# Residual loads, step order and a power on GpSimd at the seam between a mamba layer and an attention layer

## The chip, the cores and the metric

The kernel runs on 1 core of a Trainium2 chip. The metric is the device time in microseconds (us) of one execution. Engines in the profile: PE (TensorE: matmuls; PEld its weight loads), DVE (VectorE), ACT (ScalarE), POOL (GpSimd), SP (SyncE, which here only issues DMAs). Each engine works through its own queue in the order in which the program lists its instructions; between engines, semaphores order them.

## The reference, cut to what matters

Input `x` is 8 images of 128 channels and 64 x 64 pixels, in float32; an image is 4096 tokens of 128 numbers. Two layers are computed.

```
# layer 0: a mamba block, then group norm, silu and the residual
t = tokens(x); t = mamba(t)
x = silu(group_norm(image(t))) + x
# layer 1: additive attention, then a mixture of experts
t = tokens(x)
t = t + attn(layernorm(t))     # w[i,j] = exp(sum_a w2[a] tanh(f[i,a]+g[j,a]+b1[a]) + b2), j < i, normalised over j
t = t + moe(layernorm(t))      # each of 64 experts takes its 8 best tokens of an image
```

`layernorm` subtracts the mean of a token's 128 numbers and multiplies by (variance + 1e-5) to the power -0.5.

## The kernel before, in words

The work is cut into 64 chunks of 512 tokens, 8 an image (`NC` is 64, `NCH` is 8). Instructions run in the order in which the program is written (a manual schedule), so the order of the calls is the order on every queue.

**Mamba** (`mamba`) is a software pipeline over chunks: step p works on up to nine chunks in different stages. Late stages of a chunk c, which matter here, are: `normal` (group norm and silu on `o`), `again` (L434: a DMA that loads the input chunk once more, as the residual `xr`, 256 KB, two buffers), `turn` (L446, L449: transposes of `o` and of `xr` on PE, added in PSUM), `taken` (L456: ACT copies the sum to `tt`, two buffers), `moments` (L460 stores `tt` to `k_dram` by SP; L465 to L468 are the statistics on DVE), `spread` (L472, L473: logarithm and exponential on ACT, which make the power -0.5), `centre` (L478, DVE), `tokens` (L490, DVE, makes the normalised `tok`, two buffers; L486 the same on ACT for earlier chunks), `turn_back` (PE transposes `tok` back, L501 ACT copies that to `xT`, L502 a small POOL memset sets a column of `tok` to one), `vectors` (L507 stores `tok` to `k_dram` by SP; L516 two matmuls; L518 to L520 two exponentials and a scaled copy on ACT, which make `uv`) and `save` (L523: `uv` to `uv_dram`, 768 KB, by SP).

**The passage**: when the last chunk has left the scan, `remaining` (L559 to L576) finishes the late stages of the last chunks, steps p = 68 to 78. In step p, c5 to c10 are chunks p - 11 and p - 12 to p - 15. In three of the steps it calls `bring(0, g)`, which loads what attention needs of chunk g of image 0: sixteen DMAs of 64 KB for `U` and `V` (L826, L827) and two of 256 KB for `tt` and `tok` (L831). For the first three chunks the sixteen are issued by POOL, else by SP. `aw` is attention's pool of buffers, `mw` that of mamba; they share memory.

**Attention** (`attend`) walks 1056 tiles of keys by queries, 132 an image. Iteration i has several tiles in flight: `rounds` (L718, 32-row matmuls into denominators D of tile i+3 and numerators N of tile i), `logarithms` (L728, L729: ACT takes the logarithm of D), `inverses` (L735: one ACT exponential over tile i+2's reciprocals and tile i-1's scores), `ratios` (L740, three DVE products), `scores` (L753 on DVE, then L754 on POOL, whose sum L735 exponentiates in the next iteration), `causal` (L746, a mask on POOL), `weigh` (L766, matmuls). Work on finished rows (`finish`, `route`, `choose`) is written as generators that yield an engine kind and a cost; `advance` lets a few steps of them run in each iteration, between `causal` and `scores` for those on DVE and ACT. `route` calls `normalise`, once a chunk (64 times): L792 to L796 are the statistics on DVE, L798 and L799 the logarithm and the exponential on ACT (128 x 4 numbers), L802 applies them in later steps on DVE. After the tile loop come the experts and the output.

Of the kernel before, what the change touches and what calls it, by code (L numbers as in the profile page):

```python
# [9 lines left out]
F32 = mybir.dt.float32  # L10
AF = mybir.ActivationFunctionType
ALU = mybir.AluOpType
AX = mybir.AxisListType

P = 128
CH = 512
# [46 lines left out]
def fast_path(  # L63
# [24 lines left out]
    nc = tc.nc  # L88
    B = x.shape[0]
    L = x.shape[2] * x.shape[3]  # L90
    NCH = L // CH
    NB = L // P
    NQ = CH // P
    NC = B * NCH
    xf = x.rearrange("b c h w -> b c (h w)")
# [7 lines left out]
    def fixed(name, *shape):  # L103
        return const.tile(list(shape), F32, name=name)

    ident, ones = fixed("ident", P, P), fixed("ones", P, P)
# [8 lines left out]
    gamma, beta, gateb = fixed("gamma", P, 1), fixed("beta", P, 1), fixed("gateb", P, 1)  # L115
    wuv, biasv, wcol = fixed("wuv", P, 2, P), fixed("biasv", P, 1), fixed("wcol", P, 1)
    back, shift, tiny = fixed("back", P, P + 1), fixed("shift", P, 1), fixed("tiny", P, 1)
    floor = fixed("floor", P, 1)
    gwide = fixed("gwide", P, 3 * NE)

    def halves(queue, t, src):
# [2 lines left out]
    def prepare(mw, bank):  # L124
# [33 lines left out]
        spread = mw.tile([P, 2, NR, CH], F32, tag="rep", bufs=2, name="prep_spread")  # L158
        spread = spread.rearrange("p r n t -> p (r n t)")[:NS, : NS * P].rearrange("p (a r) -> p a r", a=NS)
# [55 lines left out]
        nc.vector.tensor_scalar(tiny, tiny, 1e-10, None, ALU.mult)  # L215
        nc.vector.memset(shift, -SHIFT)
        nc.vector.memset(floor, EPS)
        nc.vector.tensor_reduce(gsel, ident.rearrange("p (g c) -> p g c", c=GROUP), AX.X, ALU.add)
        nc.vector.tensor_scalar(
            gmean3, gsel.unsqueeze(2).to_broadcast([P, P // GROUP, GROUP]), 1.0 / GROUP, None, ALU.mult  # L220
# [9 lines left out]
    k_dram = [dram.tile([2, P, CH], F32, name=f"k_dram{c}", tag=f"k{c}") for c in range(NC)]  # L230
# [9 lines left out]
    def mamba(mw, small, psum):  # L240
# [5 lines left out]
        ch = [{} for _ in range(NC)]  # L246
# [255 lines left out]
            nc.gpsimd.memset(k[:, :, P - 1 : P], 1.0)  # L502
            ch[c]["ones"] = k

        def vectors(c, late=None):
            xT = ch[c].pop("xT")
            nc.sync.dma_start(k_dram[c][1], ch[c].pop("ones").rearrange("p q c -> p (q c)"))  # L507
            if late is None:
                puv = psum.tile([P, 2, CH], F32, tag="pz", name=f"puv{c}")
                puv = [puv[:, s, :] for s in range(2)]  # L510
                uv = mw.tile([P, 3, CH], F32, tag="uv", bufs=1, name=f"uv{c}")
            else:
                puv = [psum.tile([P, CH], F32, tag=f"px{s}", name=f"puv{c}_{s}") for s in range(2)]
                uv = late.tile([P, 4, CH], F32, tag="mix", bufs=5, name=f"uv{c}")[:, :3]
            for s in range(2):
                nc.tensor.matmul(puv[s], lhsT=wuv[:, s, :], rhs=xT, start=True, stop=True)  # L516
            ch[c]["uv"] = uv
            nc.scalar.activation(uv[:, 0, :], puv[0], AF.Exp, bias=shift)  # L518
            nc.scalar.activation(uv[:, 1, :], puv[1], AF.Exp, bias=biasv)
            nc.scalar.activation(uv[:, 2, :], uv[:, 1, :], AF.Copy, scale=wcol)  # L520

# [33 lines left out]
        def on(c, step, *args):  # L555
            if c is not None:
                step(c, *args)

        def remaining(aw, bring):  # L559
            for p in range(NC + 4, NC + NCH + 7):  # L560
                c5, c7, c8, c9, c10 = (
                    p - i if 0 <= p - i < NC else None for i in (NCH + 3, NCH + 4, NCH + 5, NCH + 6, NCH + 7)
                )
                if p > NC + 4:
                    on(c10, save)
                on(c8, moments)
                on(c8, spread)
                on(c8, centre)
                on(c8, tokens)
                on(c9, vectors, aw)  # L570
                on(c7, turn)
                on(c7, taken)
                on(c8, turn_back)
                on(c5, again)
                if p % 2 == 0 and p - NC - 4 < 6:
                    bring(0, (p - NC - 4) // 2)  # L576

        setup = prepare(mw, lambda h, name: psum.tile([P, CH], F32, tag=f"da{h}", name=name))
        load(0)
        next(setup)  # L580
        load(1)
        for p in range(NC + 4):

            c1, c2, c3, c4, c5, c7, c8, c9, c10 = (
                p - i if 0 <= p - i < NC else None
                for i in (0, 1, 2, 3, NCH + 3, NCH + 4, NCH + 5, NCH + 6, NCH + 7)
            )
# [63 lines left out]
            nc.scalar.preload_act_table_set(LOG_EXP)  # L651
            on(c8, turn_back)
            on(c9, vectors)
            next(setup, None)
        save(NC + 3 - (NCH + 6))
        return remaining

    def attend(aw, small, ap, remaining):
# [20 lines left out]
        U, V, tok, tt, lnf = {}, {}, {}, {}, {}  # L679
# [104 lines left out]
        def normalise(n, src, dst):  # L784

            st = small.tile([P, NQ, 6], F32, tag="st", name=f"st{n}")
            mv = small.tile([P, NQ, 2], F32, tag="lmv", name=f"lmv{n}")
            rs = small.tile([P, NQ], F32, tag="rs", name=f"rs{n}")
            for q in range(NQ):
                if q:  # L790
                    yield "v", 0.2
                nc.vector.bn_stats(st[:, q, :], src[:, q, :])  # L792
            yield "v", 0.45
            for q in range(NQ):
                nc.vector.bn_aggr(mv[:, q, :], st[:, q, :])
            nc.vector.tensor_scalar(rs, mv[:, :, 1], EPS, None, ALU.add)  # L796
            yield "end", 0.0
            nc.scalar.activation(rs, rs, AF.Ln)  # L798
            nc.scalar.activation(rs, rs, AF.Exp, scale=-0.5)  # L799
            for q in range(NQ):  # L800
                yield "v", 0.26
                nc.vector.tensor_scalar(  # L802
                    dst[:, q, :], src[:, q, :], mv[:, q, 0:1], rs[:, q : q + 1], ALU.subtract, ALU.mult
                )
# [10 lines left out]
        def bring(b, g):  # L815


            n = f"{b}_{g}"
            c = b * NCH + g
            u = U[b, g] = aw.tile([P, 2, CH], F32, tag="U", bufs=4, name=f"U{n}")  # L820
            v = V[b, g] = aw.tile([P, 2, CH], F32, tag="V", bufs=NCH + 1, name=f"V{n}")
            queue = nc.gpsimd if c < 3 else nc.sync
            for ab, to, at in ((0, 0, 64), (0, 64, 0), (1, 0, 96), (1, 64, 32)):
                for which in range(2):
                    rows = slice(to + 32 * which, to + 32 * (which + 1))
                    queue.dma_start(u[rows, ab, :], uv_dram[c][0, at : at + 32, :])  # L826
                    queue.dma_start(v[rows, ab, :], uv_dram[c][1 + which, at : at + 32, :])  # L827
            t = tt[b, g] = aw.tile([P, NQ, P], F32, tag="tt", bufs=NCH, name=f"tt{n}")
            k = tok[b, g] = aw.tile([P, NQ, P], F32, tag="tok", bufs=NCH + 1, name=f"tok{n}")
            for r, dst in enumerate((t, k)):  # L830
                nc.sync.dma_start(dst.rearrange("p q c -> p (q c)"), k_dram[c][r])  # L831
# [29 lines left out]
        def route(b, g):  # L861
            n = f"{b}_{g}"
            yield "v", 0.2
            if g == 0:
                m[b] = (
                    aw.tile([P, NCH, 2 * P], F32, tag="m", name=f"m{b}"),
                    small.tile([P, NCH, TOPK], F32, tag="cand", name=f"cand{b}"),
                )
            f = lnf[b, g] = aw.tile([P, NQ, P], F32, tag="lnf", bufs=NCH + 1, name=f"lnf{n}")
            yield from normalise(f"f{n}", tt[b, g], f)  # L870
            x = aw.tile([P, CH], F32, tag="xT", bufs=2, name=f"xf{n}")
            yield from transposed(f"f{n}", f, x)
            for k in range(NQ):
                yield "next" if k else "p", 0.36
                if k == 0:
                    pl = bank(f"pl{n}")
                i, h = divmod(k, 2)
                nc.tensor.matmul(
                    pl[:, ts(i, P)],
                    lhsT=gwide[:, ds((1 - h) * NE, P)],  # L880
                    rhs=x[:, ts(2 * h + i, P)],
                    start=h == 0,
                    stop=h == 1,
                )
            yield "free", 0.4
            logits, cand = m[b]
            nc.vector.tensor_scalar(logits[:, g, :], pl[:, : 2 * P], gateb, None, ALU.add)
            yield "v", 0.35
            nc.vector.max(cand[:, g, :], logits[:, g, :])
# [1101 lines left out]
def conv_attn_hybrid_kernel(tc, *args):  # L1991
    holds = fast_path(tc, *args)
    with tc.If(holds < 1):
        general_path(tc, *args)
# [46 lines left out]
```

## Time and profile before

| what | value |
|---|---|
| median of 4 runs | 5215.35 us (5213.42 to 5217.7) |
| the profiled execution | 5215.38 us |
| its span, first to last instruction | 5213.7 us |
| PE busy | 4951.6 us (95%) |
| ACT busy | 4895.2 us (94%) |
| DVE busy | 4643.8 us (89%) |
| POOL busy | 2048.2 us (39%) |
| mamba up to its last step | about 0 to 1469 us |
| the passage (`remaining`) | about 1469 to 1531 us |
| attention's tile loop | about 1531 to 5016 us |
| experts and output | the rest |

A line of a group of instructions reads: line, engine, operation, output<-inputs with partitions x elements and type, xcount | busy us, mean ns of one | idle time of the engine just before them, and what ended most of it. A line of a timeline reads: start us, duration us, engine, line, operation, output<-inputs, xcount, and in brackets the idle time before it and what ended it. Ends of matmuls are modelled.

### The profile page before, as it was taken

To read this page: it belongs to the slowest core of one execution; us is meant where nothing else is said; L and a number is where in the kernel's file an instruction comes from. 1 tells how busy PE (TensorE), PEld (TensorE's weight loads), DVE (VectorE), ACT (ScalarE), POOL (GpSimd) and SP (SyncE) were. 2 spreads that over 40 slices of the span, in tenths; PEclk is the share of its full clock that TensorE was granted. 3 is DMA by queue.
4 is the path that set the end of the run, shared out by engine and by line. 5 is a ranking of instruction groups with operands and counts; after the bars stand their busy time and mean duration, and the time that the engine had idled before them with its cause. 6 is when DMAs were issued, how large, how long until landed. Compare 5 with 4: busy or idle time off the path is not lost. (4 is left out here: it accounts for less than half of the span.)

```text
span 5213.7 us, 80416 instructions
## 1 busy us (share of the span) xinstructions
PE 4951.6 (95%) x27566; PEld 2261.5 (43%) x27566; DVE 4643.8 (89%) x8307; ACT 4895.2 (94%) x5750; POOL 2048.2 (39%) x1888
## 2 busy tenths in 40 slices
PE   7899999999979999999999999999999999999987
PEld 2344444444334434444444444444444444444443
DVE  8999999999939989899999999989999999998962
ACT  7899999999969999999999999999999999999962
POOL 3444444444424444344344444434433444443421
PEclk9999999999989999999999999999999999999999
DMA  2244444444451111101111111110111110111049
GB/s 98 90 143 149 150 151 157 158 158 156 138 192 33 29 39 34 37 24 48 38 29 42 53 28 40 34 37 26 46 38 29 43 52 26 43 28 57 21 173 355
DMA packets 203364, 420.74 MB, mean 81 GB/s; under 512 B 52210, under 2 KB 52866, under 8 KB 192962
## 3 DMA queue, kind: packets, MB, share of 16 engines
q1 hardware_dynamic: 192146, 394.39, 23.4%
q0 software_dynamic: 10240, 20.73, 1.1%
q8 instruction: 220, 3.60, 0.3%
q14 instruction: 198, 1.62, 0.1%
q10 hardware_dynamic: 560, 0.39, 0.0%
HBM read 291.45 MB, written 123.47 MB: 80 GB/s over the span
## 5 line engine op out<-in xcount | busy, mean ns | idle before, releaser
L740 DVE TENSOR_TENSOR mix<-mix,N 128x512 f32<-128x512 f32 x3168 | 2046.8, 684 | 285.5 <-PE N L718 181.8
L718 PE MATMUL D<-U,V 32*128 32x512 f32 (+3 forms) x9216 | 2115.3, 577 | 86.1 <-ACT mix L728 54.8
L754 POOL TENSOR_TENSOR mix<-mix 128x512 f32<-128x512 f32 x1056 | 1350.0, 1278 | 2077.0 <-DVE mix L753 1569.7
L718 PE MATMUL N<-U,V 32*128 32x512 f32 (+3 forms) x9216 | 2120.3, 576 | 0.0
L735 ACT ACTIVATE mix<-mix 128x2048 f32<-128x2048 f32 (+1 forms) x1059 | 2046.5, 1933 | 11.6 <-POOL mix L754 7.9
L718 PEld LDWEIGHTS D<-U,V 32*128 32x128 f32 x9216 | 842.9, 184 | 818.6 <-ACT mix L728 362.8
L766 PE MATMUL av<-mix,tok 128*128 128x512 f32 (+3 forms) x2304 | 1188.2, 604 | 8.4 <-DVE sums L777 5.3
L728 ACT ACTIVATE mix<-D 128x1024 f32<-128x1024 f32 x1056 | 1100.8, 1042 | 32.2 <-PE N L718 22.6
L718 PEld LDWEIGHTS N<-U,V 32*128 32x128 f32 x9216 | 842.4, 184 | 27.7 <-DVE mix L740 10.5
L753 DVE TENSOR_TENSOR mix<-mix 128x512 f32<-128x512 f32 x1056 | 724.9, 687 | 15.9
L766 PEld LDWEIGHTS av<-mix,tok 128*128 128x128 f32 x2304 | 350.6, 188 | 738.4 <-issue 646.4
L729 ACT ACTIVATE mix<-D 128x512 f32<-128x512 f32 x1056 | 650.8, 616 | 0.0
L397 POOL TENSOR_TENSOR hc<-hs,rep 128x1024 f32<-128x1024 f32 (+1 forms) x256 | 512.6, 2023 | 267.8 <-issue 172.7
L388 DVE TENSOR_TENSOR_SCAN hs<-da,hs,db 128x512 f32<-128x512 f32 x336 | 412.2, 1270 | 8.3 <-ACT da L375 3.1
L405 PE MATMUL py<-hc,ident 128*128 128x512 f32 x768 | 354.1, 597 | 0.0
L375 ACT ACTIVATE da<-dt,aneg 128x512 f32<-128x512 f32 x384 | 255.9, 692 | 37.2 <-DVE hs L388 36.4
L268 PE MATMUL px<-xt,wtap 128*128 128x512 f32 x512 | 271.8, 657 | 6.9 <-DVE wtap L137 6.9
L405 PEld LDWEIGHTS py<-hc,ident 128*128 128x128 f32 x768 | 148.3, 193 | 190.0 <-issue 188.5
L379 DVE TENSOR_TENSOR db<-dx,rep 128x1024 f32<-128x1024 f32 x192 | 229.0, 1220 | 0.0
L304 POOL DMA_DIRECT2D bc_dram<-bc x128 | 69.1, 544 | 371.7 <-ACT bc L302 371.7
L268 PEld LDWEIGHTS px<-xt,wtap 128*128 128x128 f32 x512 | 97.1, 199 | 150.3 <-issue 143.4
L279 PE MATMUL pz<-xt,wgate 128*128 128x512 f32 x256 | 128.3, 624 | 28.4 <-DVE y L361 23.5
(280 smaller groups left out, 5081.9 us busy)
## 6 DMA issues: line engine op xcount, KB each, us to landing
rep<-bc_dram SPq DMA_DIRECT2D x64, 1536.0 KB, 7.5
uv_dram<-uv SPq DMA_DIRECT2D x64, 768.0 KB, 9.4
w<-in_L_ffn_weight_dram SPq DMA_DIRECT2D x128, 256.0 KB, 5.4
U<-uv_dram SPq DMA_DIRECT2D x488, 64.0 KB, 2.0
V<-uv_dram SPq DMA_DIRECT2D x488, 64.0 KB, 2.0
xr<-in_x_dram SPq DMA_DIRECT2D x64, 256.0 KB, 8.0
k_dram<-tt SPq DMA_DIRECT2D x64, 256.0 KB, 7.8
k_dram<-tok SPq DMA_DIRECT2D x64, 256.0 KB, 9.4
```

The costliest lines, as they stand in the source:

```text
L268: nc.tensor.matmul(px, lhsT=wtap[:, tap, ts(h, P)], rhs=ch[c]["x"][:, ds(tap, CH)], start=tap == 0, stop=tap == 1,)
L388: nc.vector.tensor_tensor_scan(hs[:, h, :], ch[c].pop(("da", n, h)), db[:, h, :], first, ALU.mult, ALU.add)
L397: nc.gpsimd.tensor_tensor(hc[:, h, :], hs, ch[c]["rep"][:, 1, n, :].unsqueeze(1).to_broadcast(list(hs.shape)), ALU.mult)
L405: nc.tensor.matmul(py, lhsT=ident, rhs=ch[c]["hc", n][:, h, :], start=False, stop=n == NR - 1)
L718: nc.tensor.matmul(dst, lhsT=left, rhs=right, start=first, stop=final)
L728: nc.scalar.activation(x[:, 0:2, :], d01, AF.Ln)
L729: nc.scalar.activation(x[:, 2, :], d2, AF.Ln)
L735: nc.scalar.activation(mix[k][:, planes, :], mix[k][:, planes, :], AF.Exp, scale=-1.0)
L740: nc.vector.tensor_tensor(r[:, g, :], r[:, g, :], n[g], ALU.mult)
L753: nc.vector.tensor_tensor(r[:, 1, :], r[:, 1, :], r[:, 2, :], ALU.add)
L754: nc.gpsimd.tensor_tensor(mix[k + 1][:, 3, :], r[:, 0, :], r[:, 1, :], ALU.add)
L766: nc.tensor.matmul(av[0][:, q : q + cols], lhsT=tok[b, jb // NQ][:, jb % NQ, :], rhs=mix[t + 1][:, 3, at : at + cols], start=first and jb ...
```

## The change

Two parts. In `remaining`, the residuals of the last seven chunks are loaded at its start into seven buffers of attention's pool (tag `lnf`), the first two `bring` calls stand ahead of the steps and the third in step p = NC + 5, and the steps are put in another order: `moments` of a chunk follows its `taken` in the same step, `spread` and `centre` are called from within `vectors`, after its first exponential, and `tok` is stored (`keep`) at the end of the step, behind `save`. In `normalise`, the logarithm and exponential on ACT are replaced by one power on POOL, with a constant tile `power` of -0.5.

```diff
+    floor, power = fixed("floor", P, 1), fixed("power", P, NQ)
...
+        nc.vector.memset(power, -0.5)
...
+        def keep(c):
+            nc.sync.dma_start(k_dram[c][1], ch[c].pop("ones").rearrange("p q c -> p (q c)"))
+
-        def vectors(c, late=None):
+        def vectors(c, late=None, between=None):
             xT = ch[c].pop("xT")
-            nc.sync.dma_start(k_dram[c][1], ch[c].pop("ones").rearrange("p q c -> p (q c)"))
+            if "ones" in ch[c]:
+                keep(c)
...
             nc.scalar.activation(uv[:, 0, :], puv[0], AF.Exp, bias=shift)
+            if between is not None:
+                between()
             nc.scalar.activation(uv[:, 1, :], puv[1], AF.Exp, bias=biasv)
...
         def remaining(aw, bring):
+            for c in range(NC - NCH + 1, NC):
+                xr = ch[c]["xr"] = aw.tile([P, CH], F32, tag="lnf", bufs=NCH + 1, name=f"xr{c}")
+                nc.sync.dma_start(xr, xf[c // NCH, :, ts(c % NCH, CH)])
+            bring(0, 0)
+            bring(0, 1)
+            for step in (moments, spread, centre):
+                step(NC - NCH - 1)
             for p in range(NC + 4, NC + NCH + 7):
-                c5, c7, c8, c9, c10 = (
-                    p - i if 0 <= p - i < NC else None for i in (NCH + 3, NCH + 4, NCH + 5, NCH + 6, NCH + 7)
-                )
-                if p > NC + 4:
-                    on(c10, save)
-                on(c8, moments)
-                on(c8, spread)
-                on(c8, centre)
+                c7, c8, c9, c10 = (p - i if 0 <= p - i < NC else None for i in range(NCH + 4, NCH + 8))
+
+                def scaled():
+                    on(c7, spread)
+                    on(c7, centre)
+
                 on(c8, tokens)
-                on(c9, vectors, aw)
                 on(c7, turn)
                 on(c7, taken)
                 on(c8, turn_back)
-                on(c5, again)
-                if p % 2 == 0 and p - NC - 4 < 6:
-                    bring(0, (p - NC - 4) // 2)
+                on(c7, moments)
+                if c9 is not None:
+                    vectors(c9, aw, scaled)
+                else:
+                    scaled()
+                on(c9, save)
+                on(c8, keep)
+                if p == NC + 5:
+                    bring(0, 2)
...
             nc.vector.tensor_scalar(rs, mv[:, :, 1], EPS, None, ALU.add)
             yield "end", 0.0
-            nc.scalar.activation(rs, rs, AF.Ln)
-            nc.scalar.activation(rs, rs, AF.Exp, scale=-0.5)
+            nc.gpsimd.tensor_tensor(rs, rs, power, ALU.pow)
```

More of the change, by code (lines that the diff above doesn't have):

```diff
@@ L117, in fast_path @@
     back, shift, tiny = fixed("back", P, P + 1), fixed("shift", P, 1), fixed("tiny", P, 1)
-    floor = fixed("floor", P, 1)
+    floor, power = fixed("floor", P, 1), fixed("power", P, NQ)
     gwide = fixed("gwide", P, 3 * NE)
```

## The prediction

> **What bounds the kernel now.** I read the busy shares on the page first: PE 95% and ACT 94%, so the page alone doesn't decide. The change touches two stages, and each is read from its own rows: the tile loop of attention (1560 to 5000 us of the span) and the passage between the two layers (1469 to 1531 us).
>
> In the tile loop the costliest groups of ACT between 1700 and 4800 us:
>
> ```profile
> L735 ACT ACTIVATE mix<-mix 128x2048 f32<-128x2048 f32 x944 | 1829.5, 1938 | 4.5 <-POOL mix L754 1.2
> L728 ACT ACTIVATE mix<-D 128x1024 f32<-128x1024 f32 x943 | 983.6, 1043 | 23.1 <-PE N L718 21.2
> L729 ACT ACTIVATE mix<-D 128x512 f32<-128x512 f32 x943 | 581.8, 617 | 0.0
> L798 ACT ACTIVATE rsf<-rsf 128x4 f32<-128x4 f32 x55 | 11.7, 212 | 0.0
> L799 ACT ACTIVATE rsf<-rsf 128x4 f32<-128x4 f32 x55 | 11.4, 207 | 1.7
> ```
>
> Before every group there is almost no idle time: ACT is busy 3408.9 of the 3440 us from 1560 to 5000 (99.1%). PE waits for it: the list of waits gives 362.8 us in which a weight load of L718 waits for ACT L728. ACT sets the pace of this loop; what is taken from ACT is gained, up to the next limit. One iteration with the two operations of `normalise`, from ACT's timeline:
>
> ```profile
> 1583.34 1.03 ACT L728 ACTIVATE mix<-D 128x1024 f32<-128x1024 f32 x1
> 1584.24 0.61 ACT L729 ACTIVATE mix<-D 128x512 f32<-128x512 f32 x1
> 1584.72 1.93 ACT L735 ACTIVATE mix<-mix 128x2048 f32<-128x2048 f32 x1
> 1586.52 0.23 ACT L798 ACTIVATE rsf<-rsf 128x4 f32<-128x4 f32 x1
> 1586.77 0.21 ACT L799 ACTIVATE rsf<-rsf 128x4 f32<-128x4 f32 x1
> 1586.89 1.01 ACT L728 ACTIVATE mix<-D 128x1024 f32<-128x1024 f32 x1
> ```
>
> From L728 to L728 it takes 3.55 us; without the pair 1586.89 to 1590.07, 3.18. The pair costs 0.35 us of ACT, all on the path.
>
> In the passage no engine is full: from 1475 to 1515 ACT is busy 22.3 of 40 us, PE 28.2, DVE 17.0, while the mean DMA share is 1.00 at 340 GB/s. PE's and ACT's timelines show why:
>
> ```profile
> 1493.11 0.48 PE L449 MATMUL pt<-ident,xr 128*128 128x128 f32 x1 [3.90 <-DMA xr<-in_x_dram]
> 1511.54 0.33 PE L449 MATMUL pt<-ident,xr 128*128 128x128 f32 x1 [1.87 <-DMA xr<-in_x_dram]
> 1517.58 0.33 PE L449 MATMUL pt<-ident,xr 128*128 128x128 f32 x1 [1.80 <-DMA xr<-in_x_dram]
> ```
>
> ```profile
> 1481.47 0.59 ACT L456 COPY tt<-pt 128x512 f32<-128x512 f32 x1 [0.26 <-PE pt L449]
> 1482.00 0.59 ACT L501 COPY xT<-pb 128x512 f32<-128x512 f32 x1
> 1483.48 0.21 ACT L472 ACTIVATE rs<-rs 128x4 f32<-128x4 f32 x1 [0.89 <-DVE rs L468]
> ```
>
> A residual `xr` is asked for one step before its use and comes late three times (3.90 + 1.87 + 1.80 = 7.6 us). And in each of eight steps ACT stands still for 0.6 to 0.9 us before L472, because `moments` (L465 to L468, 1.4 us of DVE) only begins after the copy L456 of the step before.
>
> **The change, part by part.**
>
> *Power on POOL.* Removed: 64 pairs on ACT. What is late next is PE: in iterations without the pair, the last matmul of L718 ends 0.06 us (median of 968) before L728 starts; with the pair 0.40 us before. So a removed pair gives at most 0.35 us and no more than its PE slack less 0.05. Summed over the 63 pairs in the loop this is 18.9 us (a quarter give under 0.04, because there PE already binds). The 64th pair is in the tail: DVE waits 0.51 us for it at 5023 us; a POOL operation takes its place, I count 0.
>
> Added: one POOL operation on 128x4, waiting for DVE L796. Queued behind it on POOL is the addition L754, and for that waits ACT L735 of the next iteration. DVE and POOL in the same iteration:
>
> ```profile
> 1585.14 0.17 DVE L796 TENSOR_SCALAR rsf<-lmvf 128x4 f32<-128x4 f32 x1
> 1585.22 0.68 DVE L753 TENSOR_TENSOR mix<-mix 128x512 f32<-128x512 f32 x1
> ...
> 1586.07 1.28 POOL L754 TENSOR_TENSOR mix<-mix 128x512 f32<-128x512 f32 x1 [1.62 <-DVE mix L753]
> ```
>
> L754 has to wait for L753 anyway, which ends 0.6 us after L796. If the power runs beside L753, those 0.6 us hide it. But does it? In mamba POOL's 128x1024 product L397 takes 3.20 us when it starts at 1404.26, beside DVE's L379 with two inputs in SBUF (1404.04 to 1405.24), and 2.35 us when nothing of that kind runs: it lost 0.85 of the 0.98 us that they overlap. So I count the power as starting only when L753 ends: L754 comes later by the whole power. The Trainium skill ("SBUF — State Buffer", Who interferes with whom) says that a DVE instruction with two SBUF inputs and a GpSimd instruction that reads SBUF exclude each other for the whole instruction, the later one blocking fully; by it nothing of the power hides under L753, and without it up to 0.6 us would.
>
> Room before ACT feels it, from the end of L753 plus power plus 1.28 us to L735 already moved 0.35 us forward, over the 63 pairs: 0.29 us in a quarter of them, 0.69 at the median, 1.01 in the best tenth. Summing what exceeds the room: a power of 0.3 us loses 0.2 in all (18.7 gained), 0.4 us 2.3 (16.6), 0.6 us 6.5 (12.4), 0.8 us 12.5 (6.4), 0.95 us about nothing left, 1.28 us about 39 (20 lost).
>
> No power is in the trace. Lower end: POOL's smallest operation that reads SBUF, the 16x5 selection, 0.19 us. Upper end: its two-input operation on 512 elements, L754, 1.28 us. By size (4 elements a partition) it is nearest to the first; a power is more arithmetic than a selection, so I take twice that, 0.4 us. 16.6 us, less some 2 us for DVE, which runs without a gap in these iterations (L740 to L740 3.07 and 3.16 us at 3566 to 3572) and must now do its work in 3.2 us instead of 3.55: **14.5 us gained**.
>
> *Residuals at once.* Seven loads of 256 KB go to SP behind the save of chunk 53 (issued 1469.25). The three waits of 7.6 us go. What is late next: the same queue now carries 7 x 256 KB plus `tt` and `tok` of rows 0 and 1 (4 x 256 KB) ahead of the first store of `tt` (chunk 55), which must land before the copy of chunk 57 can use that buffer (two buffers). With chunk 53's 0.77 MB that is about 3.9 MB. Up to 404 GB/s were moved (1495 to 1505); POOL's own DMAs take some 100 of them (64 KB in 0.65 us), and at 300 the store lands 13 us after 1469.3, at about 1483; the copy of chunk 57 was at 1481.5 before. **About 2 us given back.**
>
> *First rows at once.* 32 issues on POOL, at 0.50 us and with waits for landings 10.4 us per sixteen (1476.80 to 1487.20), can start after the memset at 1458.5, where DMA is nearly idle (share 0.00 from 1458 to 1469), and end about 1481. That pulls some 1.3 of 3.1 MB out of the crowded stretch. Behind them on POOL is the memset of chunk 55 (1473.4 before), for which SP's store of `tok` waits, and behind that SP's later stores. The third row's sixteen issues then sit between the memsets of chunks 56 and 57 and hold the second by some 9 us. Before, SP waited 13.2 us in three pieces for such memsets (L507 after POOL L502); I count **3 us** that reach the chain through the two `tok` buffers (such waits of DVE L490 were 0.9 to 1.6 us each, four times).
>
> *Order of steps.* `moments` of a chunk comes directly after its copy, and its logarithm and exponential sit between two exponentials of `vectors`: ACT's 0.6 to 0.9 us before L472 is filled with L518. Eight times, 7.1 us in all, of which I count **6 us**. A step then is ACT's own 3.6 us (copy 0.5, copy 0.5, L518 to L520 2.2, pair 0.35), lengthened by the matmuls that L518 needs to about 4.3 us; the best steps before took 4.5 (1481.47 to 1486.01). The stores of `tok` move behind those of `uv`: 768 KB, 2 us, within the two-step life of a buffer. After the copy of chunk 63 before took 12.1 us (1518.6 to 1530.7); now moments, pair, tokens, transposes, copy and two `vectors` give about 10, counted within the 6.
>
> Passage: 7.6 + 6 - 2 - 3 = 8.6, **9 us gained**. Both ends: nothing gained if the DMA queue, full already, just moves the waits; about 16 if no stall replaces the old ones (7 x 4.3 + 10 us after the first copy at 1473 makes 1513 instead of 1530.7, so 17 at the very most).
>
> The memset of `power` at the start is one more DVE instruction under a mamba step: 0.
>
> **Sum.** The profiled execution took 5215.38 us, 1.7 over its span, and equals the median (5215.35) of the runs shown. 5215.4 - 14.5 - 9 = **5192 us**.
>
> **The rivals.**
>
> *Power is long on POOL (slower).* POOL's L754 starts after it, ACT waits for L754. It decides at 0.95 us, where attention gains nothing, and the whole is slower from about 1.1 us. At 1.28 us attention loses 20, with the passage's 9 that is 5226; each further 0.1 us costs 6. For it: nothing in the trace shows POOL computing a power. Against: its per-element rate (1.28 us for 512) makes four elements nearly free. I give 0.26.
>
> *The passage's waits only change their name.* DMA share is 1.00 there; the two `tt` and `tok` buffers, SP's order and POOL's memsets take over. Then 0 of 9, total 5201. For it: the full queue. Against: the queue idles before 1469 and the residuals are waited for by PE directly. 0.10.
>
> *ACT is relieved, but nothing follows.* PE ends 0.06 us before L728 already and DVE is back to back; if these two hold the pace, attention gives only a few us and the total is 5206, within the change's noise. Against: with the pair PE demonstrably stands ready 0.40 us early. 0.09.
>
> **How the numbers follow.** Forecast 0.55 (5192; its own range 5180 to 5202). Two tenths of a per cent (10.4 us) is about what a measurement of this kernel can tell from no change. Faster: 0.54 of the forecast, 0.08 of the second rival, 0.02 of the third, 0.64. Within: 0.01 + 0.02 + 0.06 and 0.04 of the long power, 0.13. Slower: 0.22 of the long power, 0.01, 0.23. The range: below, a power of 0.2 us or under (18.9) with 16 in the passage, 5180; above, into the long power a little past 1.28 us, 5228.
>
> **What would show it.** Right: L728 to L728 in the iterations with L796 at 3.18 to 3.25 us instead of 3.55; ACT's wait before L735 for POOL L754 still some us in all; no wait of PE L449 for `xr`; the first matmul of L718 near 1520 instead of 1529.2. Wrong: a POOL operation at L815 of 1 us or more with L735 waiting for L754 right behind; or PE, DVE or SP waits in the passage that add up to the old ones (a copy of chunk 57 much after 1483, L490 waiting for stores).

## The result and the profile after

The changed kernel takes 5223.14 us (median of 32 runs, 5215.61 to 5229.74) beside 5217.06 us for the kernel before (52 runs, 5210.36 to 5222.35). The ratio is 1.0011, with an interval of 1.0006 to 1.0016: about 6 us slower, where 23 us faster was forecast. The profiled execution took 5222.27 us, its span is 5220.5.

I cut both traces into the same four stages. The marks are the end of the last group norm in mamba, ACT's first logarithm of attention (L728 before, L745 after), its ninth, and its last.

| stage, us | before | after |
|---|---|---|
| mamba, to the end of the last group norm | 1464.9 | 1469.6 |
| passage, to the first logarithm of attention | 66.4 | 72.4 |
| start, to the ninth logarithm | 31.9 | 30.6 |
| tile loop, ninth to last logarithm | 3439.4 | 3436.9 |
| tail | 211.0 | 211.0 |

The 4.7 us of mamba are not the change's. In the traces of this study the mark lies between 1464.9 and 1470.4 us, for kernels that differ in nothing before it as well (1464.9 here and 1468.7 in no_power below); so the lengths of the other stages are compared. What is left is a loop that gained 2.5 us where 14.5 were counted, and a passage that lost 6.0 where 9 were to be gained.

These are lengths in single traces. The loop's is steady: 3438.1 to 3439.4 us in the seven kernels of this study that have the loop of before. The passage's is not: 63.4 to 66.4 us in the five that have the passage of before, in part because the mark moves. The ninth logarithm, counted from the start of the span, starts at 1562.9 to 1567.5 us in these five (the middle one at 1563.7) and at 1572.6 in the changed kernel. By that the passage lost some 9 us, and with the 2.5 of the loop this comes closer to the measured 6 than the stages alone do.

**The loop.** The groups of ACT between 1700 and 4800 us, in the kernel after. The pair of L798 and L799 is gone, and ACT's other groups are as long as before:

```profile
L752 ACT ACTIVATE mix<-mix 128x2048 f32<-128x2048 f32 x944 | 1828.4, 1937 | 13.0 <-POOL mix L771 9.1
L745 ACT ACTIVATE mix<-D 128x1024 f32<-128x1024 f32 x944 | 984.1, 1043 | 25.7 <-PE N L735 24.5
L746 ACT ACTIVATE mix<-D 128x512 f32<-128x512 f32 x944 | 581.6, 616 | 0.0
```

Read the end of the first line: the exponential stood still for 13.0 us, 9.1 of them for POOL's addition L771; before, it was 4.5 and 1.2. The groups of POOL in the same stretch name the cause:

```profile
L771 POOL TENSOR_TENSOR mix<-mix 128x512 f32<-128x512 f32 x944 | 1206.4, 1278 | 1709.4 <-DVE mix L770 1277.5 <-PE N L735 342.9 <-ACT mix L752 64.2
L815 POOL TENSOR_TENSOR rsf<-rsf,power 128x4 f32<-128x4 f32 x54 | 75.0, 1389 | 54.8 <-DVE rsf L813 54.8
```

A power of 128 x 4 numbers takes POOL 1389 ns, longer than its addition of 128 x 512 numbers (1278). One case out of the timelines of POOL, DVE and ACT, in that order:

```profile
2666.03 1.39 POOL L815 TENSOR_TENSOR rsf<-rsf,power 128x4 f32<-128x4 f32 x1 [1.12 <-DVE rsf L813]
2667.39 1.27 POOL L771 TENSOR_TENSOR mix<-mix 128x512 f32<-128x512 f32 x1
```

```profile
2665.78 0.17 DVE L813 TENSOR_SCALAR rsf<-lmvf 128x4 f32<-128x4 f32 x1
2665.86 0.69 DVE L770 TENSOR_TENSOR mix<-mix 128x512 f32<-128x512 f32 x1
```

```profile
2668.70 1.91 ACT L752 ACTIVATE mix<-mix 128x2048 f32<-128x2048 f32 x1 [0.44 <-POOL mix L771]
```

DVE's sum L770 is done at 2666.55, but POOL is in the power until 2667.42. The addition ends at 2668.66, and ACT has waited 0.44 us for it. Over the 63 cases of the loop, the iteration that had the pair fell from a mean of 3.70 to 3.40 us, as it does in no_power below, and the next one rose from 3.19 to 3.44.

**The passage.** The list of waits between 1469 and 1542 us, its entries for DMAs. In the kernel before, PE waited 7.6 us for residuals and DVE 5.2 us for stores of `tok`:

```profile
DVE tok L491 <- DMA k_dram<-tok: 22.4, 5, 13.8
ACT tt L457 <- DMA k_dram<-tt: 10.5, 1, 10.5
...
PE pt L450 <- DMA xr<-in_x_dram: 0.7, 1, 0.7
```

The residuals are no longer waited for. In their place stands one long stall for two stores, which SP's timeline explains:

```profile
1473.96 0.37 SPq L530 DMA_DIRECT2D uv_dram<-uv  x1
1477.85 3.77 SPq L569 DMA_DIRECT2D xr<-in_x_dram  x7
1481.67 0.47 SPq L847 DMA_DIRECT2D tt<-k_dram  x1
1482.18 1.02 SPq L847 DMA_DIRECT2D tok<-k_dram  x1
1483.24 0.44 SPq L847 DMA_DIRECT2D tt<-k_dram  x1
1483.78 0.38 SPq L847 DMA_DIRECT2D tok<-k_dram  x1
1485.66 1.52 SPq L461 DMA_DIRECT2D k_dram<-tt  x2
1488.31 0.54 SPq L507 DMA_DIRECT2D k_dram<-tok  x1
1490.36 0.37 SPq L530 DMA_DIRECT2D uv_dram<-uv  x1
```

and SP's own waits from 1465 to 1500 us:

```profile
SPq L569 <- DMA uv_dram<-uv: 3.3, 1, 3.3
...
SPq L461 <- DMA xr<-in_x_dram: 2.3, 2, 1.5
SPq L530 <- DMA xr<-in_x_dram: 1.4, 1, 1.4
SPq L507 <- DMA xr<-in_x_dram: 1.1, 1, 1.1
```

Three things follow each other there. The first residual, which is SP's first DMA into attention's pool, waits 3.3 us until the save of chunk 53 has landed: it is issued at 1477.85 and not behind the save at 1474.3. The two pools share memory, and that the wait comes of it is likely but not shown; POOL's loads of `U` and `V` into the same pool began at 1466.60. Then eleven loads of 256 KB go out ahead of the first store. And stores wait for landings of loads that they have nothing to do with: the store of `tt` at 1485.66 for that of the fourth residual, eight DMAs earlier on the same queue, at 1485.64. It lands at 1493.5. ACT and DVE wait for that and for the store of `tok` behind it:

```profile
1493.58 0.59 ACT L457 COPY tt<-pt 128x512 f32<-128x512 f32 x1 [10.54 <-DMA k_dram<-tt]
```

```profile
1494.94 1.11 DVE L491 TENSOR_SCALAR tok<-tt,rs,at 128x128 f32<-128x128 f32 x4 [13.83 <-DMA k_dram<-tok]
```

The two waits are one stall seen from two engines. The stretches from 1480 to 1500 us show it too: ACT is busy 4.45 of 20 us there, with PE at a granted clock of 0.50; before, 10.33 of 20 at 0.93 and 0.59.

### The profile page after: what moved, and what is told of

Read it like the earlier page. It is cut to its first block, busy times and chain, and to the rows that moved or that the text cites. A ratio compares the mean times of both kernels' runs of the same rounds, so it can differ in the third digit from the quotient of the medians.

```text
span 5220.5 us, 80487 instructions
## 1 busy us (share of the span) xinstructions
PE 4952.2 (95%) x27566; PEld 2263.6 (43%) x27566; DVE 4643.1 (89%) x8308; ACT 4880.6 (93%) x5622; POOL 2135.1 (41%) x1952
## 5 line engine op out<-in xcount | busy, mean ns | idle before, releaser
L771 POOL TENSOR_TENSOR mix<-mix 128x512 f32<-128x512 f32 x1056 | 1349.5, 1278 | 1924.1 <-DVE mix L770 1456.7
L745 ACT ACTIVATE mix<-D 128x1024 f32<-128x1024 f32 x1056 | 1100.1, 1042 | 34.0 <-PE N L735 28.0
L770 DVE TENSOR_TENSOR mix<-mix 128x512 f32<-128x512 f32 x1056 | 724.7, 686 | 15.9
```

The source lines that it names most:

```text
L745: nc.scalar.activation(x[:, 0:2, :], d01, AF.Ln)
L770: nc.vector.tensor_tensor(r[:, 1, :], r[:, 1, :], r[:, 2, :], ALU.add)
L771: nc.gpsimd.tensor_tensor(mix[k + 1][:, 3, :], r[:, 0, :], r[:, 1, :], ALU.add)
```

## The experiments

Theory A: two independent losses, a power that is too long for its place on POOL, and stores held up behind loads on SP. Rivals: the loss is in mamba (the constant tile); the new order of steps is itself bad; the loads are bad wherever they stand; in the loop PE or DVE would have held the pace anyway. Each experiment is timed against the kernel before on the same chip; where only a part of the change is in, all else is as before.

**pow_alone** and **passage_alone**: one half of the change each.

```diff
 # pow_alone: before, with
-            nc.scalar.activation(rs, rs, AF.Ln)
-            nc.scalar.activation(rs, rs, AF.Exp, scale=-0.5)
+            nc.gpsimd.tensor_tensor(rs, rs, power, ALU.pow)
 # passage_alone: the changed kernel, with these three lines the other way round
```

> The kernel before with the power on POOL as the only edit. Theory A (the passage lost, the power gained almost nothing): the tile loop is 2 to 3 us shorter, as in the changed kernel's profile (3439.4 to 3436.9 us from the 9th to the last L728), the passage is as before, so the total is 2 to 3 us under before. Theory B (the extra constant and its memset disturb mamba, which was 4.7 us longer in the changed kernel's profile): mamba up to the last group norm ends near 1469.6 instead of 1464.9 us, and the total is 2 us over before. In both the power takes 1.39 us in the loop, and L735 follows POOL's addition by 0.03 us in the iteration after it.

> The changed passage, with the logarithm and exponential left on ACT and no constant. Theory A: the passage takes 6 us more (72.4 instead of 66.4 us from the last group norm to the first L728), the start of the tile loop 1.4 us less, the loop itself 3439 us: 4 to 5 us over before. Theory B: the same, with mamba as before; then this is the dearer half of the change only if mamba's 4.7 us stay with the other half.

Measured: 5214.33 us beside 5214.72, ratio 0.9997 (0.9988 to 1.0006), and 5223.77, ratio 1.0017 (1.0008 to 1.0026). The passage carries the whole loss; a gain of the power doesn't show in the time, though an interval from 6 us under to 3 over leaves room for one. In the traces the power alone has the loop at 3435.9 us (3439.4 before) and the passage at 64.3; the passage alone has the loop at 3438.1, the passage at 72.1, and the ninth logarithm at 1570.9. The mark of mamba is at 1468.3 with the constant tile and 1465.4 without it, but at 1468.7 and 1470.3 in two later kernels that don't have it either (no_power, order_alone): the rival of mamba falls.

**no_power** takes the upper bound of the loop: it leaves the logarithm and the exponential out and puts nothing in their place, so the rows are not scaled.

```diff
-            nc.scalar.activation(rs, rs, AF.Ln)
-            nc.scalar.activation(rs, rs, AF.Exp, scale=-0.5)
```

> The kernel before with logarithm and exponential of that layer norm left out and nothing in their place, so rows are not scaled by the power. It measures the ACT term alone. Theory A: 15 to 19 us under before, the same as with the power behind the addition within 3 us. If it is under 5, PE or DVE set the pace and the prediction's 18.9 us was wrong whatever POOL does.

Measured: 5199.19 us, ratio 0.9967 (0.9955 to 0.9979), 15.5 us less than before; the loop takes 3424.5 us, 14.9 less. So ACT's relief is there to be had, PE and DVE follow, and the rival of a pace held by others falls. The same lines of ACT as above, in this kernel:

```profile
L735 ACT ACTIVATE mix<-mix 128x2048 f32<-128x2048 f32 x947 | 1833.7, 1936 | 4.6 <-POOL mix L754 1.2
L728 ACT ACTIVATE mix<-D 128x1024 f32<-128x1024 f32 x947 | 988.3, 1044 | 26.7 <-PE N L718 25.6
```

The wait for POOL is at 1.2 us as before; that for PE rose from 21.2 to 25.6, which is what PE takes back.

**pow_behind** puts the power behind the addition on POOL, with all else as in pow_alone.

```diff
-            nc.gpsimd.tensor_tensor(rs, rs, power, ALU.pow)
+            behind.append(lambda: nc.gpsimd.tensor_tensor(rs, rs, power, ALU.pow))
...
+            flush()     # in the loop, after scores
```

> The kernel before, with the power on POOL put behind POOL's addition of the same iteration instead of ahead of it. If the power loses only because the addition, and with it ACT's exponential, queues behind it: L735 waits no more, the tile loop gains the 18.9 us worked out in the prediction less what DVE holds back, 15 to 19 us in all. If PE or DVE hold the pace anyway (the third rival), the loop is no shorter than with the power ahead, 2 to 3 us. If POOL is then late for the next iteration's addition, in between.

Measured: 5217.79 us, ratio 1.0004 (0.9995 to 1.0014), with the loop at 3441.3 us. No better, though the iteration that had the pair (mean 3.41 us) and the next one (3.19) are now both short. The third rose to 3.50 us, from 3.22 before. The same chunk as above, on DVE, POOL and ACT:

```profile
2659.31 1.87 DVE L741 TENSOR_TENSOR mix<-mix,N 128x512 f32<-128x512 f32 x3
2661.85 0.86 DVE L808 TENSOR_SCALAR lnf<-tt,lmvf,rsf 128x128 f32<-128x128 f32 x3 [0.66 <-POOL rsf L805]
2662.63 0.68 DVE L754 TENSOR_TENSOR mix<-mix 128x512 f32<-128x512 f32 x1
```

```profile
2660.79 1.02 POOL L805 TENSOR_TENSOR rsf<-rsf,power 128x4 f32<-128x4 f32 x1
...
2663.46 1.27 POOL L755 TENSOR_TENSOR mix<-mix 128x512 f32<-128x512 f32 x1 [1.38 <-DVE mix L754]
```

```profile
2664.76 1.91 ACT L736 ACTIVATE mix<-mix 128x2048 f32<-128x2048 f32 x1 [0.45 <-POOL mix L755]
```

DVE has L808, which applies the result, next in its queue and waits 0.66 us for the power (24.0 us in all, in 42 of the 64 cases). Its sum, POOL's addition and ACT's exponential, queued behind, are late by it. The loss of the power moved by one iteration, from POOL's queue to DVE's.

**pow_behind_later_use** tests that reading: the application stands one iteration later.

```diff
             behind.append(lambda: nc.gpsimd.tensor_tensor(rs, rs, power, ALU.pow))
+            yield "end", 0.0
```

> The passage of before, the power on POOL behind POOL's addition (as in pow_behind), and one more pause in the generator, so that the application of rs on DVE stands an iteration later than in pow_behind. Theory W (pow_behind lost ACT's relief because DVE's application waited for a power that ended 1.0 us after the addition, 1588.89 in its trace, and DVE's next sum, POOL's next addition and ACT's next exponential were all late behind it): nothing is late any more, so about what leaving the operations out gave, -14 us (-10 to -16) against before, 5199 to 5203; the third iteration's mean goes from 3.50 us back to 3.20 to 3.26. Rival R (POOL itself is too full, whoever waits for the power): its 1.0 us still push the addition of the next iteration, the result stays within 4 us of before, 5211 to 5217, and the third or a later iteration stays at 3.4 or more.

Measured: 5204.36 us beside 5214.15, ratio 0.9984 (0.9975 to 0.9993): 9.8 us less. The third iteration is back at a mean of 3.20, and the loop takes 3427.3 us, 12.1 less than before. POOL wasn't too full; it was who waited for the power. The same chunk again, DVE and POOL:

```profile
2660.66 0.69 DVE L754 TENSOR_TENSOR mix<-mix 128x512 f32<-128x512 f32 x1
2661.39 2.11 DVE L741 TENSOR_TENSOR mix<-mix,N 128x512 f32<-128x512 f32 x3
2663.41 0.86 DVE L809 TENSOR_SCALAR lnf<-tt,lmvf,rsf 128x128 f32<-128x128 f32 x3
```

```profile
2660.22 1.02 POOL L805 TENSOR_TENSOR rsf<-rsf,power 128x4 f32<-128x4 f32 x1
```

The power runs from 2660.22 to 2661.24 and is used at 2663.41. The gain is just short of the 10 to 16 us that were expected, and 2.8 us of loop below no_power's; in which iterations they lie isn't settled.

**order_alone** and **loads_alone**: one half of the passage each.

```diff
 # order_alone: the new order of steps, but the residuals asked for
 # step by step, at the end of the step, and bring where it was
+                on(c7, moments)
...
+                on(c9, save)
+                on(c8, keep)
                 on(c5, again)
 # loads_alone: the order of before, with the seven loads of xr,
 # bring(0, 0) and bring(0, 1) ahead of the steps, bring(0, 2) in step NC + 5
```

> The kernel before with the new order of steps alone: residuals asked for one step ahead and rows brought in three steps, as before. Theory Q (the loads put ahead of the stores on SP are what cost): the order itself gains, the passage is 59 to 62 us instead of 64 to 66, 3 to 6 us under before. Rival O (the order costs, because the store of tok now stands behind the 768 KB save and its buffer comes free late): at or over before, with DVE waiting for stores of tok in every second step.

> The kernel before with the loads at the start of the passage alone, steps in the old order. Theory Q: 8 to 12 us over before, with ACT or DVE waiting some 10 us for the stores of tt and tok once, in the first two steps. Rival O: under before by the 7.6 us for which PE waited for residuals.

Measured: 5263.69 us beside 5213.13, ratio 1.0091 (1.0076 to 1.0107), and 5212.45, ratio 0.9998 (0.9989 to 1.0007). The order with residuals asked for at the end of each step costs 50 us. That is the sign of rival O, but not its reason: the waits of PE for `xr` go from 7.6 to 55.0 us, since the load of the next step's residual now stands on SP behind the save that ends this step:

```profile
1497.05 0.37 SPq L529 DMA_DIRECT2D uv_dram<-uv  x1
1497.52 0.44 SPq L506 DMA_DIRECT2D k_dram<-tok  x1
1498.04 0.94 SPq L434 DMA_DIRECT2D xr<-in_x_dram  x1
```

```profile
1502.67 0.47 PE L449 MATMUL pt<-ident,xr 128*128 128x128 f32 x1 [7.07 <-DMA xr<-in_x_dram]
```

The early loads without the new order change nothing in time: neither the 8 to 12 us over of theory Q came nor the 7.6 under of rival O. Their list of waits shows the stall of the changed kernel, smaller, in place of the 7.6 us for `xr`:

```profile
DVE tok L490 <- DMA k_dram<-tok: 11.6, 2, 11.0
ACT tt L456 <- DMA k_dram<-tt: 6.6, 1, 6.6
```

So the order is of no use with residuals that stand behind the save, and the loads, all at once, bring a stall with them. That doesn't yet tell an order that is bad from an order that isn't served.

**keep_early** and **stores_first** keep the new order and change how SP serves it; both have the pair on ACT, as before.

```diff
 # keep_early: passage_alone, with the store of tok ahead of vectors and save
                 on(c7, moments)
+                on(c8, keep)
...
                 on(c9, save)
-                on(c8, keep)
 # stores_first: as keep_early; and the stores that are ready go ahead of all loads,
 # each xr is asked for one at a time behind the step's stores, U and V
 # of rows 1 and 2 in halves, one a step, the tt and tok rows in three late steps
+            keep(NC - NCH - 2)
+            moments(NC - NCH - 1)
+            again(NC - NCH + 1)
+            bring(0, 0, rows=False)
...
+                if c6 is not None:
+                    xr = ch[c6]["xr"] = aw.tile([P, CH], F32, tag="lnf", bufs=NCH + 1, name=f"xr{c6}")
+                    nc.sync.dma_start(xr, xf[c6 // NCH, :, ts(c6 % NCH, CH)])
```

> The changed passage with one call moved: tok is stored ahead of uv and not behind it. Theory Q: the long wait at the copy of chunk 57 (10.5 us) stays, the later waits for stores of tok (2.5, 2.8, 1.7, 1.6 us) go: 3 to 5 us less than the changed passage, still 4 to 6 over before. Rival O: at or under before.

> The new order of steps with SP's queue rearranged: stores of tok and tt ahead of any load, each residual asked for two steps ahead, tok ahead of uv, POOL's sixteen issues per row cut into pieces of four DMA pairs a step, and tt and tok of the first rows loaded in the last steps. Theory Q: passage 52 to 56 us, 9 to 13 us under before. If DMA throughput over the passage sets its length whatever the order (340 GB/s of mean in the profile before), no more than 4 us under before.

Measured: 5214.96 us beside 5213.13, ratio 1.0003 (0.9994 to 1.0012), and 5204.77, ratio 0.9983 (0.9974 to 0.9992), 8.4 us less than before, just short of the 9 to 13 expected. With the store of `tok` ahead of the save the passage takes 65.5 us instead of 72.1: the later waits of DVE for `tok` (2.5, 2.8, 1.7 and 1.6 us in the changed kernel) shrink to one of 3.8, and the stall at the start stays. In stores_first that goes too, and the passage takes 55.6 us:

```profile
1471.79 0.37 SPq L529 DMA_DIRECT2D uv_dram<-uv  x1
1472.25 0.44 SPq L506 DMA_DIRECT2D k_dram<-tok  x1
1472.74 0.86 SPq L460 DMA_DIRECT2D k_dram<-tt  x1
1473.69 1.16 SPq L434 DMA_DIRECT2D xr<-in_x_dram  x1
1475.94 0.32 SPq L460 DMA_DIRECT2D k_dram<-tt  x1
```

Its waits for DMAs:

```profile
PE pt L449 <- DMA xr<-in_x_dram: 6.3, 4, 4.0
...
DVE tok L490 <- DMA k_dram<-tok: 2.1, 3, 1.2
```

So the new order isn't bad in itself: with it, and nearly the old waits for `xr`, the passage is 10.8 us shorter than before (66.4), and the ninth logarithm starts at 1556.4 us, 6.8 earlier than before. How much of that is the order's isn't shown, because stores_first changes the order, the place of the stores and the spread of the loads at once, and no run has its queue with the old order of steps.

**stores_first_three** asks for each residual a step earlier, to remove those 6.3 us.

```diff
-                if c6 is not None:
+                for c in {0: (58, 59), 1: (60,), 2: (61,), 3: (62,), 4: (63,)}.get(p - NC - 4, ()):
```

> Only the passage, as in stores_first, but two residuals are asked for in the first step (chunks 58 and 59) and one in each step after, so that each load stands one step earlier than there. Theory Q (what is left in stores_first are the waits of PE for xr, 6.0 us, of loads that were issued too late, not the rate of the DMA engines): these waits go, the passage shortens from 55.6 to 50 to 53 us, and the time is 2 to 6 us under stores_first's, a ratio to before of 0.9972 to 0.9980 (5199 to 5203). Rival D (the DMA engines are full, and every byte asked for sooner delays a store by as much): the waits change from xr to tok or tt, passage 55 to 57 us, ratio 0.998 to 0.9985 as stores_first.

Measured: 5206.08 us, ratio 0.9980 (0.9971 to 0.9989), against 0.9983 of stores_first. The waits for `xr` are gone, and those for `tok` have taken their place:

```profile
DVE tok L490 <- DMA k_dram<-tok: 7.8, 6, 2.3
```

The passage reads 52.2 us instead of 55.6, with the start of the loop behind it as long as before (33.2 beside 33.4). But the mark is later as well, 1470.4 beside 1467.5 us, and the ninth logarithm starts at 1555.7 beside 1556.4. The time, 8.1 us less than the kernel before where stores_first had 8.4, agrees: a gain over stores_first isn't shown. Theory Q is right that the waits were those of late loads, and rival D that a wait for stores takes their place and the time stays.

**both_mended** puts the two mended parts together.

```diff
 # stores_first_three, with the power of pow_behind_later_use
```

> The passage of stores_first_three and the power of pow_behind_later_use together. If both hold and add up (they lie in different stages): -9 to -13 of the passage and -10 to -16 of the loop, about -24 us against before (-19 to -29), 5189 to 5196. If only the passage holds: -8 to -13, 5202 to 5207. If only the loop holds: -6 or less beyond what pow_behind_later_use gives.

Measured: 5197.06 us beside 5214.15, ratio 0.9964 (0.9951 to 0.9978), 17.1 us less than before. Apart, the parts gave 9.8 and 8.1, so they add up; the sum is under the 24 expected because each part was. It is the fastest full kernel of the study.

## Why the prediction was wrong

**The pair on ACT, and its relief: right.** With the pair left out, 14.9 us of loop went, beside 18.9 less 2 for DVE. The iterations that had it are 3.29 us at the median, a little over the 3.18 to 3.25 that were to show. One aside of that working doesn't fit its own sum: seven of the 63 pairs, and not a quarter, give under 0.04 us; 18.9 is the sum with seven.

**The power at 0.4 us: wrong, the term that undid the loop.** It takes 1.02 us alone and 1.39 beside DVE's sum. The row to which it was likened, a selection of 16 x 5 numbers, says nothing of a power, and size said nothing either: four elements a partition take 1.02 us where the 512 of an addition take 1.28. The upper bound of the estimate, 1.28 us, was the nearer row. The rest of that working stood. It counted the power from the end of DVE's sum; measured so, it ends 0.88 us after (median of the 63 in the loop). The prediction's own table gives 6.4 us for 0.8 and none for 0.95, so some 3 for 0.88, 1 after the 2 for DVE; the loop gained 2.5. Its mechanism, ACT's next exponential behind the addition, is the one that the trace shows. What the table left open is which place is safe for a long power. It isn't simply "behind the addition": the application on DVE has to move as well.

**The port: half right.** "L754 comes later by the whole power" held nearly: of 0.51 us that the power ran beside the sum, it lost 0.37 (1.39 less 1.02). But with this power the loss is of one order only. In pow_behind_later_use the power starts first and DVE's sum second in 48 cases: the sum takes 0.69 us, its usual time, and the power 1.02. The Trainium skill ("SBUF — State Buffer", SBUF: two separate sides) has the one that starts first hold the port for the whole instruction and the other block fully; by it DVE's sum would have been late there by up to 0.67 us, and in no case was it. Longer operations of POOL do hold DVE. In mamba of the kernel before, on DVE and POOL:

```profile
68.27 2.15 DVE L411 TENSOR_TENSOR y<-y,zs 128x1024 f32<-128x1024 f32 x1
```

```profile
66.85 2.49 POOL L397 TENSOR_TENSOR hc<-hs,rep 128x512 f32<-128x512 f32 x2
```

DVE's product with both inputs in SBUF starts second, 1.07 us before the end of POOL's, and takes 2.15 us where 1.22 is its usual time: there DVE loses most of the overlap.

**The waits for `xr` (-7.6): right.** 0.7 us are left of them.

**About 2 us given back by the first store: the step that undid the passage.** The copy of chunk 57 came 16.5 us after the mark before and 23.9 after it now, 7.4 us later and not 2. The first store of `tt` landed 19.6 us after the issue of chunk 53's save, where 13 were counted, and two things in the sum were off. The loads couldn't go "behind the save of chunk 53": they had to wait for its landing, 3.3 us. And a store that is ready wasn't issued when the queue reached it, but when the DMA eight places ahead of it had landed, 1.5 us and 0.8 us more for the first two. The rate was less far off: 289 GB/s from 1480 to 1490 us beside the 300 counted; from 1470 to 1480 it was 214, but SP's loads only began at 1477.85. Only the stall's beginning was in the sum; that the store of `tok` stands still further behind, and holds DVE to 1494.94, was not.

**The store of `tok` behind `save`, "2 us, within the two-step life of a buffer": wrong.** The steps that follow the stall wait 2.5, 2.8, 1.7 and 1.6 us for it. Putting it back ahead of the save is worth 6.6 us of the passage (keep_early beside passage_alone), and about 7 in time: 1.8 us above before instead of 9.1.

**POOL's early issues, and 3 us for the memsets: the first right, the second not seen.** The 32 issues ran from 1466.60 to 1483.08 us, 16.5 us where 22.5 were counted, and the memset came at 1483.07. The store of `tok` that needs it wasn't held by it (in the whole passage SP waited 0.2 us for such memsets, beside 13.2 before): SP came to that store only at 1487.2, when the two stores of `tt` were out.

**The order of steps (-6): its mechanism right, its size not shown.** ACT's wait for the statistics, which it was to fill, went from 7.1 us before to 0.7 in the changed kernel (L472 and L473 behind DVE). But what that is worth depends on residuals that are early and stores that are prompt: with residuals asked for late the order costs 50 us, and in stores_first, where the passage is 10.8 us shorter, it isn't measured apart from them. The prediction added the parts as if each stood by itself.

Of the rivals, the long power came true in length (1.39 us) but not in price: in the rival's own terms, from the end of DVE's sum, it is 0.88 us, short of the 0.95 at which it decides, and the loop still gained 2.5 us. That the passage's waits only change their name came true beyond its bound of "0 of 9". The time, 5223, lies within the range of 5180 to 5228, but by luck: the upper end was reckoned from a power that costs 20 us beside a passage that gains 9, and what took the time there is the passage. What failed is alike in both parts: I took a time from an amount (four elements, 3.9 MB). In the loop the queue behind the power was counted and the power itself was short by more than half; in the passage the bytes were about right, and the waits for landings ahead of the first store, and the store of `tok` behind it, were missing.

## What to carry to other kernels

An operation that the trace doesn't show is priced by its upper row until it has been measured, if the queue behind it is on the path; and moving it further back helps only if its reader moves back too. Loads that are early take the place of stores in the same queue: before many are asked for at once, count what stands behind them, and let stores that free a buffer go first, the loads one at a time. A new order of steps and an early load can each be worth nothing or less, and together, with the stores first, 8 us, so parts of a change are to be tried apart and in their better form before either is dropped.

## What the runs showed of the hardware

- POOL's power of 128 x 4 numbers took 1.007 to 1.04 us in all cases where no DVE sum was under way at its start, and 1.39 (median) where one was; its addition of 128 x 512 takes 1.28. DVE's product with one input in PSUM (L741), under way at the start in 63 cases of pow_behind, doesn't lengthen it.
- A DVE sum with both inputs in SBUF that starts during POOL's power is not lengthened (0.69 us, 48 cases, up to 0.67 us beside each other), nor is the power (1.01 to 1.04). That doesn't hold the other way round, nor for a longer operation of POOL: beside a product of 128 x 512, DVE's L411 took 2.15 us instead of 1.22.
- In these kernels an issue on SP waits for the landing of the DMA eight before it: in the changed kernel SP issued at 1485.66 us, when the residual issued at 1479.18 had landed at 1485.64. Of the 1802 DMAs that SP issues there, none starts before that landing where the trace has it, and 97 start within 0.08 us behind it; 119 start before the landing of the one seven before. Whether this is the chip's or the program's doing isn't shown.
- The granted TensorE clock was 0.50 through the stall (1470 to 1500 us) and 0.91 in the 20 us behind it; before, it was 0.93 from 1480 to 1490 and 0.59 from 1490 to 1500. What that cost wasn't measured by itself.
